# A mixture of experts whose first product keeps the weights in the array and streams the tokens

## The chip, the cores and the metric

The kernel runs on one NeuronCore of a Trainium2 chip. The metric is the device time of one execution in microseconds (us), as the median of several runs. A profile, taken from one further execution, gives the start and duration of every instruction on the core's engines: TensorE (PE, with its weight loads listed apart as PEld), VectorE (DVE), ScalarE (ACT), GpSimd (POOL) and the queue of SyncE that issues DMAs (SP).

## The reference: what is computed

The input `x` is 4 x 1024 tokens of 256 float32 values. Four layers follow one another, each added to `x` after a layer norm: a retention layer (16 heads), a mixture of experts, an RWKV layer (a recurrence over 1024 tokens), and the same mixture again, with the same weights. The change is in the mixture:

```python
logits = t @ Wg.T + bg                      # 4096 tokens, 8 experts
probs = softmax(logits); topw, topi = top_k(probs, 2)
topw = topw / sum(topw)
for e in range(8):
    h = t @ w1[e].T                         # 256 -> 512
    gate, up = split(h, 2)                  # 256 each
    a = silu(gate) * up
    o = a @ w2[e].T                         # 256 -> 256
    out += combine[:, e] * o                # 0 for tokens that did not choose e
```

All of it is float32.

## The kernel before, in words

**Pages.** The kernel computes the mixture only for the experts that a token chose. Each of the 2 x 4096 (token, expert) pairs gets a slot in a table in DRAM (`xg_all`), sorted by expert, in pages of 128 slots; a page belongs to one expert. There are `NSL = 71` pages per mixture: 64 full ones and 7 more, since each expert's last page may be partly empty. `Piece.route` computes the slots on DVE in several steps. `Piece.send` (line 792) normalizes 128 tokens on ACT and writes each of them to its two slots by two indirect DMAs that POOL issues. A mixture is routed in pieces of the batch, and its first `FULL = 25` pages can be worked off before the later pieces have been sent; page 25 and those behind it need every send.

**One page** `j` goes through these steps in class `Moe`:

- `get` (827): SP loads up to four pages of slots into `m_xg`.
- `fetch` (838): PE transposes the page's 128 x 256 tokens in two blocks into `m_xtp` (PSUM), and ACT copies them to `m_xt`, so that channels lie on partitions.
- `expert` (906): PE loads the number of the page's expert from `m_ofi` into a register. In the profile this is TENSOR_LOAD, FUSED_REGOPS and SEQ_ASSERT on PE's queue.
- `up` (848): the first product. The tokens (`m_xt`, two blocks of 128 channels) are the stationary operand, loaded into the array, and the expert's weights, 512 columns of `w1a` that the register points to, are the moving one. `m_hp` has tokens on partitions and the 512 hidden units along the row. ACT takes silu of the first half (`m_sg`), DVE multiplies it by the second half into `m_a`. For the first page of each group of four, DVE also computes from the tags of the slots their shares (`m_share`) and the rows that they go to (`m_to`), in seven small operations.
- `turn` (878): PE transposes `m_a` in two blocks into `m_atp`, and DVE copies it to `m_aT`, so that hidden units lie on partitions.
- `down` (885): the second product, with `m_aT` stationary and 256 columns of `w2a` moving, into `m_op`, which has one PSUM buffer that it shares with another tile (tag `yp`). ACT scales it by the share into `m_y`.
- `scatter` (896): POOL issues an indirect DMA that writes the page's 128 rows to `y_all` in DRAM.

**Order.** `tiles` (909) writes out by hand the order on PE, ACT, DVE and POOL: in iteration `j` it fetches page `j + 2`, does `up(j)`, loads the expert of `j + 1`, turns `j - 2` and does `down(j - 4)`. SP's order is left to a scheduler. `extra[j]` holds work of the neighbouring layers that is put behind iteration `j`: the ends of retention, routing and sends of the later pieces, the inputs of RWKV (from `FULL + 24` on), and, once the pages that hold a block of tokens have been scattered, `ask` (938) and `take` (950): SP loads the two rows of each token from `y_all` into `m_back`, and DVE adds them to `x` (line 954). The functions `back_to` and `add` set their iterations. Scatters are held back in the list `late`: POOL has a budget of seven DMA issues for three iterations, sends go first, and at most `LAG = 8` pages wait (lines 927 to 935). `m_y` has `LAG + 4` buffers.

**Numbers of instructions.** Each float32 matmul of the program stands in the profile as two MATMUL and two LDWEIGHTS; a transpose stands as one of each. So `m_hp` has 142 pages x 2 blocks x 2 = 568, `m_op` 568, `m_atp` and `m_xtp` 284 each.

Of the kernel before, what the change touches and what calls it, by code (L numbers as in the profile page):

```python
# [62 lines left out]
HB = NBLK // 2  # L63
HT = HB * NT
FULL = 2 * HT - E + 1
LAG = 8

W = C + 4
N_OUT = 2 * TT * P
# [40 lines left out]
def hybrid_kernel(  # L110
# [693 lines left out]
    class Moe:  # L804


        def __init__(self, layer, pieces):
            self.layer = layer
            self.xg, self.to, self.ev, self.xt, self.act, self.aT = {}, {}, {}, {}, {}, {}
            self.rows, self.share, self.ofi, self.ofs = {}, {}, {}, []  # L810
            self.y, self.late = {}, []
            self.slots = tc.dram_tile([NSL * P, W], F32, name=f"xg_all{layer}")
            *self.sends, self.early = dram_disjoint_views(self.slots, 2 * TT + 1)
            self.results = tc.dram_tile([N_OUT + NSL * P, C], F32, name=f"y_all{layer}")
            *self.scatters, self.back = dram_disjoint_views(self.results, NSL + 1)
            self.pieces, n = [], 0
            for k in pieces:
                self.pieces.append(Piece(self, n, k, self.pieces[-1] if n else None))
                n += k

            self.groups = [(0, 1)] + [
                (lo, min(GRP, end - lo)) for start, end in ((1, FULL), (FULL, NSL))
                for lo in range(start, end, GRP)]
            self.group = {lo + i: (g, i) for g, (lo, n) in enumerate(self.groups) for i in range(n)}
# [21 lines left out]
            nc.scalar.copy(self.xt[j], tp)  # L846

        def up(self, j):
            hp = psum([P, DFF], "m_hp")
            for c in range(KC):  # L850
                mm(hp, lhsT=self.xt[j][:, c, :],  # L851
                   rhs=w1a[:, bass.ds(self.ev[j], 1), c, :].rearrange("p o n -> p (o n)"),
                   start=(c == 0), stop=(c == KC - 1))
            sg = px.tile([P, C], F32, name="m_sg", tag="m_sg", bufs=2)
            nc.scalar.activation(sg, hp[:, 0:C], AF.Silu)  # L855
            self.act[j] = px.tile([P, C], F32, name="m_a", tag="m_a", bufs=3)
            nc.vector.tensor_mul(self.act[j], hp[:, C : 2 * C], sg)  # L857
            g, i = self.group[j]
            if i == 0:
                n = self.groups[g][1]  # L860
# [14 lines left out]
                    second, tags[:, :, 0], 0.0, second, ALU.is_gt, ALU.mult)  # L875
                nc.vector.tensor_add(to[:, 0:n], second, void[:, j : j + n])

        def turn(self, j):
            tp = px2.tile([P, KC, P], F32, name="m_atp", tag="m_atp", bufs=2)
            for c in range(KC):  # L880
                nc.tensor.transpose(tp[:, c, :], self.act[j][:, c * P : (c + 1) * P], ident)  # L881
            self.aT[j] = px.tile([P, KC, P], F32, name="m_aT", tag="m_aT", bufs=3)
            nc.vector.tensor_copy(self.aT[j], tp)

        def down(self, j):
            op = psum([P, C], "m_op", "yp")
            for c in range(KC):
                mm(op, lhsT=self.aT[j][:, c, :],  # L888
                   rhs=w2a[:, bass.ds(self.ev[j], 1), c, :].rearrange("p o n -> p (o n)"),
                   start=(c == 0), stop=(c == KC - 1))  # L890
            g, i = self.group[j]
            y = self.y[j] = px.tile([P, C], F32, name="m_y", tag="m_y", bufs=LAG + 4)
            nc.scalar.activation(y, op, AF.Copy, scale=self.share[g][:, i : i + 1])  # L893
            self.late.append(j)
# [11 lines left out]
        def expert(self, j):  # L906
            self.ev[j] = nc.tensor.value_load(self.ofi[j], min_val=0, max_val=E - 1)

        def tiles(self, extra):


            spent = 0
            self.fetch(0)
            self.fetch(1)
            self.expert(0)
            for j in range(NSL + 4):
                if j + 2 < NSL:
                    self.fetch(j + 2)
                if j < NSL:
                    self.up(j)  # L920
                if j + 1 < NSL:
                    self.expert(j + 1)
                if 0 <= j - 2 < NSL:
                    self.turn(j - 2)
                if j > 3:
                    self.down(j - 4)
                spent = max(spent, 7 * j // 3)
                for f, *a in extra.get(j, ()):
                    f(*a)
                    spent += 2 * (f.__name__ == "send")  # L930
                while self.late and (spent < 7 * (j + 1) // 3 or len(self.late) > LAG):
                    self.scatter()
                    spent += 1
            while self.late:
                self.scatter()
# [665 lines left out]
    def back_to(moe, pieces):  # L1601

        for p in pieces:
            lo, hi = p.start * NT, p.start * NT + p.nt
            start = 2 * hi + E - 1 + 4
            for i in range(lo, hi):
                add(start + i - lo, moe.ask, i)
                add(start + 2 + i - lo, moe.take, i)
# [25 lines left out]
    add(FULL + 4, inputs)  # L1634
    back_to(moe, moe.pieces[:1])
    for n in range(-1, 8):
        add(FULL + 25 + 3 * n if n >= 0 else FULL + 24, lambda n: made["rwkv"][0](n), n)
    moe.tiles(extra)
    pi, w = made["pi"], made["w"]
    prepare, wstep, finish = made["rwkv"]  # L1640
# [208 lines left out]
```

## Time and profile before

| | |
|---|---|
| median of 3 runs | 1552.75 us (1551.82 to 1554.12) |
| the profiled execution | 1556.23 us |
| its span, first to last instruction | 1554.3 us |
| mean granted TensorE clock | 0.925 |
| first `m_hp` of the first mixture, last of its `m_hp` pages | 346.4, 630.8 us |
| first `m_hp` of the second mixture, last of its `m_hp` pages | 1265.5, 1528.5 us |
| `m_a` on DVE (line 857) | 142 x 423 ns |
| `m_aT` on DVE (line 883) | 142 x 415 ns |
| `y_all` scatter on POOL (line 900) | 142 x 969 ns |
| `xg_all` send on POOL (line 798) | 128 x 978 ns |

How to read it: a line of the profile names the source line, the engine, the operation, the tiles as out<-in, and the count; behind the bar stand busy us and mean ns, and behind the second bar the idle time of that engine just ahead of these instructions, with what ended it. In a timeline the first two numbers are the start and the duration in us, both from the start of the span; what stands in brackets is the idle time ahead and its releaser. A timeline line with x4 covers four instructions, from the start of the first to the end of the last. A stage's line begins with its window and length, has the busy us of PE, PEld, DVE, ACT and POOL with their instructions, and ends with the granted clock, the DMA share and GB/s.

### The profile page before, as it was taken

To read this page: it belongs to the slowest core of one execution; us is meant where nothing else is said; L and a number is where in the kernel's file an instruction comes from. 1 tells how busy PE (TensorE), PEld (TensorE's weight loads), DVE (VectorE), ACT (ScalarE), POOL (GpSimd) and SP (SyncE) were. 2 spreads that over 40 slices of the span, in tenths; PEclk is the share of its full clock that TensorE was granted. 3 is DMA by queue.
4 is the path that set the end of the run, shared out by engine and by line. 5 is a ranking of instruction groups with operands and counts; after the bars stand their busy time and mean duration, and the time that the engine had idled before them with its cause. 6 is when DMAs were issued, how large, how long until landed. Compare 5 with 4: busy or idle time off the path is not lost.

```text
span 1554.3 us, 20957 instructions
## 1 busy us (share of the span) xinstructions
PE 1313.1 (84%) x6704; PEld 675.9 (43%) x6704; DVE 1004.7 (65%) x1963; ACT 648.7 (42%) x1649; POOL 891.2 (57%) x854
## 2 busy tenths in 40 slices
PE   5999998877879999997878888888787567979995
PEld 3666665544445655422222323233222124546663
DVE  6667567426533344399978797989998956433454
ACT  2343434433533334445445454545445234523332
POOL 4232322742564335399998888887799923553332
PEclk9999999878989999999989898999898779989998
DMA  8992111231432341267655453534554831333564
GB/s 296 329 330 74 56 55 42 81 115 53 132 115 87 114 139 62 72 149 195 164 135 149 122 145 99 145 99 122 136 162 136 248 107 48 104 105 99 159 207 159
DMA packets 117546, 207.71 MB, mean 134 GB/s; under 512 B 12192, under 2 KB 80000, under 8 KB 117440
## 3 DMA queue, kind: packets, MB, share of 16 engines
q1 hardware_dynamic: 95904, 160.22, 36.1%
q0 software_dynamic: 17184, 39.86, 8.2%
q10 hardware_dynamic: 4352, 6.29, 1.3%
q8 instruction: 57, 0.93, 0.3%
q14 instruction: 49, 0.40, 0.1%
HBM read 139.19 MB, written 67.14 MB: 133 GB/s over the span
## 4 chain that ended last, share of the span: by engine, by line
PE 57%; DVE 14%; POOL 11%; ACT 8%; issue 5%; DMA 2%; another core or an unknown queue 2%; POOLq 0%; SPq 0%; DVEq 0%; ACTq 0%
PE m_hp L851 15%; PE m_op L888 7%; PE w_pp L1108 5%; POOL w_s L1204 5%; DVE w_s L1196 4%; PE a_qkp L315 3%; PE a_yp L374 2%; DVE w_vb L1194 2%; PE m_xtp L844 2%; PE w_dp L1056 2%; PE a_op L249 2%; PE a_sp L354 2%; PE a_gp L297 2%; PE m_atp L881 2%; POOL w_xf L1074 2%
## 5 line engine op out<-in xcount | busy, mean ns | idle before, releaser
L1204 POOL TENSOR_TENSOR w_s<-w_s,w_rT 128x1024 f32<-128x1024 f32 x128 | 303.9, 2411 | 38.9 <-DVE w_s L1196 27.8
L851 PE MATMUL m_hp<-w1a,m_xt 128*128 x568 | 283.2, 623 | 3.8 <-DVE m_a L857 3.8
L900 POOL DMA_INDIRECT y_all<-m_y,m_to x142 | 137.5, 969 | 211.8 <-ACT m_xt L846 145.4
L857 DVE TENSOR_TENSOR m_a<-m_hp,m_sg 128x256 f32<-128x256 f32 x142 | 60.1, 423 | 266.2 <-ACT m_sg L855 239.5
L798 POOL DMA_INDIRECT xg_all<-m_row,m_at x128 | 125.2, 978 | 100.0 <-ACT m_row L796 42.9
L1196 DVE TENSOR_TENSOR_SCAN w_s<-w_wk,w_carry,w_vb 128x512 f32<-128x512 f32 x128 | 161.0, 1276 | 17.3 <-PE w_yp L1227 5.1
L888 PE MATMUL m_op<-w2a,m_aT 128*128 x568 | 150.8, 389 | 19.5 <-ACT m_y L893 13.7
L1194 DVE TENSOR_TENSOR w_vb<-w_vb,w_wk 128x1024 f32<-128x1024 f32 x128 | 153.3, 1198 | 18.8 <-ACT w_wk L1137 17.6
L1196 DVE TENSOR_TENSOR_SCAN w_s<-w_wk,w_vb 128x512 f32<-128x512 f32 x128 | 152.9, 1216 | 13.2 <-POOL w_sx L1027 3.0
L851 PEld LDWEIGHTS m_hp<-w1a,m_xt 128*128 128x128 f32 x568 | 102.4, 200 | 79.0 <-issue 74.2
L1227 PE MATMUL w_yp<-w_s,core_c 128*32 128x512 f32 x512 | 92.3, 645 | 47.7 <-POOL w_s L1204 38.0
L855 ACT ACTIVATE m_sg<-m_hp 128x256 f32<-128x256 f32 x142 | 54.5, 384 | 169.4 <-PE m_hp L851 119.3
L888 PEld LDWEIGHTS m_op<-w2a,m_aT 128*128 128x128 f32 x568 | 98.7, 194 | 31.5 <-ACT m_y L893 17.2
L893 ACT ACTIVATE m_y<-m_op,m_share 128x256 f32<-128x256 f32 x142 | 67.2, 473 | 107.3 <-PE m_op L888 84.4
L327 POOL TENSOR_TENSOR a_t<-a_t,a_t 128x512 f32<-128x512 f32 x32 | 41.0, 1281 | 118.3 <-DVE a_t L326 95.9
L1074 POOL TENSOR_TENSOR w_xf<-w_xf,w_sx 128x512 f32<-128x512 f32 x60 | 77.8, 1297 | 40.5 <-ACT w_xf L1073 39.5
L357 DVE TENSOR_TENSOR a_pt<-a_sp,ret_c 128x2048 f32<-128x2048 f32 x32 | 73.2, 2286 | 16.9 <-PE a_sp L354 16.9
L881 PEld LDWEIGHTS m_atp<-cst,m_a 128*128 128x128 f32 x284 | 40.6, 144 | 79.6 <-issue 67.8
L1077 POOL TENSOR_TENSOR w_xf<-w_xf,w_xT 128x512 f32<-128x512 f32 x64 | 69.7, 1090 | 5.4 <-DVE w_xf L1071 0.7
L844 PE MATMUL m_xtp<-cst,m_xg 128*128 128x128 f32 x284 | 58.3, 289 | 13.5 <-DMA m_xg<-xg_all 13.3
L846 ACT COPY m_xt<-m_xtp 128x256 f32<-128x256 f32 x142 | 51.9, 366 | 37.8 <-PE m_xtp L844 22.4
L1227 PEld LDWEIGHTS w_yp<-w_s,core_c 128*32 128x32 f32 x512 | 14.2, 113 | 112.4 <-POOL w_s L1204 59.4
(312 smaller groups left out, 2496.7 us busy)
## 6 DMA issues: line engine op xcount, KB each, us to landing
w_vb<-v_all SPq DMA_DIRECT2D x125, 512.0 KB
xg_all<-zero SPq DMA_DIRECT2D x34, 520.0 KB
m_xg<-xg_all SPq DMA_DIRECT2D x34, 520.0 KB
tab<-in_rope SPq DMA_DIRECT2D x32, 512.0 KB
m_back<-y_all SPq DMA_DIRECT2D x48, 256.0 KB
v_all<-w_vT SPq DMA_DIRECT2D x64, 128.0 KB
res<-in_x SPq DMA_DIRECT2D x8, 512.0 KB
w1a<-in_w SPq DMA_DIRECT2D x8, 512.0 KB
```

What stands on the lines that cost most here:

```text
L357: nc.vector.tensor_mul(pts[i].rearrange("p j n t -> p (j n) t"), sp.rearrange("p j n t -> p (j n) t"), causal.unsqueeze(1).to_broadcast([P ...
L798: nc.gpsimd.indirect_dma_start(out=self.moe.sends[2 * (self.start * NT + i) + n][:, :], out_offset=bass.IndirectOffsetOnAxis(ap=self.at[n] ...
L844: nc.tensor.transpose(tp[:, c, :], self.xg[g][:, i, c * P : (c + 1) * P], ident)
L851: mm(hp, lhsT=self.xt[j][:, c, :], rhs=w1a[:, bass.ds(self.ev[j], 1), c, :].rearrange("p o n -> p (o n)"), start=(c == 0), stop=(c == KC - 1))
L888: mm(op, lhsT=self.aT[j][:, c, :], rhs=w2a[:, bass.ds(self.ev[j], 1), c, :].rearrange("p o n -> p (o n)"), start=(c == 0), stop=(c == KC - 1))
L900: nc.gpsimd.indirect_dma_start(out=self.scatters[j][:, :], out_offset=bass.IndirectOffsetOnAxis(ap=self.to[g][:, i : i + 1], axis=0), in_= ...
L1074: nc.gpsimd.tensor_mul(xf, xf, sx)
L1108: mm(pp, lhsT=w[n][:, c, m * P : (m + 1) * P], rhs=d["xf", f][:, c, :], start=(c == 0), stop=(c == KC - 1))
L1194: nc.vector.tensor_mul(vb, vb, wk[:, 1:2, :].to_broadcast([P, 2, BLK]))
L1196: nc.vector.tensor_tensor_scan(s[:, q, 1 : BLK + 1], wk[:, 0, :], vb[:, q, :], 0.0 if j % NB == 0 else st[j - 1]["carry"][:, n, 2 * h + q ...
L1204: nc.gpsimd.tensor_mul(s[:, :, 0:BLK], s[:, :, 0:BLK], d["r"][:, g, :].unsqueeze(1).to_broadcast([P, 2, BLK]),)
L1227: mm(d["yp", g][32 * q : 32 * q + 32, :], lhsT=w["sel"][:, i, :], rhs=d["s", n, q // 2][:, q % 2, 0:BLK], start=False, stop=(i == 3), skip ...
```

## The change

The expert's 256 x 512 weights become the stationary operand of the first product, in eight blocks of 128 x 128, and the page's tokens are streamed. The output `m_hp` then has hidden units on partitions (4 blocks of 128 units x 128 tokens), and `m_a` can go into the second product as it is: `turn`, `m_atp` and `m_aT` are gone. The stationary blocks are read from a copy of the expert's weights at a fixed address: for each page the new `first` loads the expert's number into a register of DVE, and DVE copies that expert's weights, 128 x 1024 float32, from `w1a` into `m_w1` (three buffers). `tiles` calls it for page `j + 2` in iteration `j`, ahead of `up(j)`, and for pages 0 and 1 ahead of the loop. `down` comes two iterations after `up`, not four, and `m_op` gets two PSUM buffers of its own, where `m_atp` had them. `LAG` is 6, so `m_y` has 10 buffers, and the iterations of `ask`, `take` and of RWKV's preparation move two earlier.

```diff
-LAG = 8
+LAG = 6
...
         def up(self, j):
-            hp = psum([P, DFF], "m_hp")
-            for c in range(KC):
-                mm(hp, lhsT=self.xt[j][:, c, :],
-                   rhs=w1a[:, bass.ds(self.ev[j], 1), c, :].rearrange("p o n -> p (o n)"),
-                   start=(c == 0), stop=(c == KC - 1))
-            sg = px.tile([P, C], F32, name="m_sg", tag="m_sg", bufs=2)
-            nc.scalar.activation(sg, hp[:, 0:C], AF.Silu)
-            self.act[j] = px.tile([P, C], F32, name="m_a", tag="m_a", bufs=3)
-            nc.vector.tensor_mul(self.act[j], hp[:, C : 2 * C], sg)
+
+            hp = psum([P, DFF // P, P], "m_hp")
+            for m in range(DFF // P):
+                for c in range(KC):
+                    mm(hp[:, m, :],
+                       lhsT=self.w1[j][:, c, m * P : (m + 1) * P],
+                       rhs=self.xt[j][:, c, :], start=(c == 0), stop=(c == KC - 1))
+            sg = px.tile([P, KC, P], F32, name="m_sg", tag="m_sg", bufs=2)
+            nc.scalar.activation(sg, hp[:, 0:KC, :], AF.Silu)
+            self.act[j] = px.tile([P, KC, P], F32, name="m_a", tag="m_a", bufs=3)
+            nc.vector.tensor_mul(self.act[j], hp[:, KC : 2 * KC, :], sg)
...
-        def turn(self, j):
-            tp = px2.tile([P, KC, P], F32, name="m_atp", tag="m_atp", bufs=2)
+        def down(self, j):
+            op = px2.tile([P, 512], F32, name="m_op", tag="m_op", bufs=2)[:, 0:C]
             for c in range(KC):
-                nc.tensor.transpose(tp[:, c, :], self.act[j][:, c * P : (c + 1) * P], ident)
-            self.aT[j] = px.tile([P, KC, P], F32, name="m_aT", tag="m_aT", bufs=3)
-            nc.vector.tensor_copy(self.aT[j], tp)
-
-        def down(self, j):
-            op = psum([P, C], "m_op", "yp")
-            for c in range(KC):
-                mm(op, lhsT=self.aT[j][:, c, :],
+                mm(op, lhsT=self.act[j][:, c, :],
                    rhs=w2a[:, bass.ds(self.ev[j], 1), c, :].rearrange("p o n -> p (o n)"),
                    start=(c == 0), stop=(c == KC - 1))
...
+        def first(self, j):
+
+            e = nc.vector.value_load(self.ofi[j], min_val=0, max_val=E - 1)
+            self.w1[j] = px.tile([P, KC, DFF], F32, name="m_w1", tag="m_w1", bufs=3)
+            nc.vector.tensor_copy(
+                self.w1[j], w1a[:, bass.ds(e, 1), :, :].rearrange("p o c n -> p (o c) n"))
+
         def tiles(self, extra):
...
             self.expert(0)
-            for j in range(NSL + 4):
+            self.first(0)
+            self.first(1)
+            for j in range(NSL + 2):
                 if j + 2 < NSL:
                     self.fetch(j + 2)
+                if j + 2 < NSL:
+                    self.first(j + 2)
                 if j < NSL:
                     self.up(j)
                 if j + 1 < NSL:
                     self.expert(j + 1)
-                if 0 <= j - 2 < NSL:
-                    self.turn(j - 2)
-                if j > 3:
-                    self.down(j - 4)
+                if j > 1:
+                    self.down(j - 2)
...
-            start = 2 * hi + E - 1 + 4
+            start = 2 * hi + E - 1 + 2
...
-        add(FULL + 25 + 3 * n if n >= 0 else FULL + 24, lambda n: made["rwkv"][0](n), n)
+        add(FULL + 23 + 3 * n if n >= 0 else FULL + 22, lambda n: made["rwkv"][0](n), n)
```

More of the change, by code (lines that the diff above doesn't have):

```diff
@@ L808, in __init__ @@
             self.layer = layer
-            self.xg, self.to, self.ev, self.xt, self.act, self.aT = {}, {}, {}, {}, {}, {}
+            self.xg, self.to, self.ev, self.xt, self.act = {}, {}, {}, {}, {}
             self.rows, self.share, self.ofi, self.ofs = {}, {}, {}, []
-            self.y, self.late = {}, []
+            self.y, self.w1, self.late = {}, {}, []
             self.slots = tc.dram_tile([NSL * P, W], F32, name=f"xg_all{layer}")
```

## The prediction

> **What bounds the kernel now.** I read the page's table of engines first, then its groups, then busy time by stage, then the timeline of one page of the mixture.
>
> ```profile
> PE 1313.1 (84%) x6704; PEld 675.9 (43%) x6704; DVE 1004.7 (65%) x1963; ACT 648.7 (42%) x1649; POOL 891.2 (57%) x854
> ...
> L851 PE MATMUL m_hp<-w1a,m_xt 128*128 x568 | 283.2, 623 | 3.8 <-DVE m_a L857 3.8
> ```
>
> TensorE (PE) is busiest and the edited product, m_hp, is its largest group. The share of the whole span says little, because the middle of the span (RWKV) is not touched. The two mixtures run at 342 to 640 us and 1262 to 1540 us. Their quiet halves are these two windows (after the time, busy us of PE, PEld, DVE, ACT, POOL):
>
> ```profile
> 474.00:640.00 166.00, 163.15 (x607) 94.41 (x608) 69.46 (x236) 63.26 (x159) 70.27 (x81) 0.99 0.31 98
> 1388.00:1540.00 152.00, 148.00 (x587) 91.31 (x585) 71.22 (x240) 55.65 (x148) 49.31 (x52) 1.00 0.48 152
> ```
>
> PE never rests there, at full granted clock (1.00, 0.99), while VectorE (DVE) is under half busy. By the starts of m_hp the windows hold 45 and 47 of the 142 pages. One page on PE's timeline:
>
> ```profile
> 521.16 0.38 PE L881 MATMUL m_atp<-cst,m_a 128*128 128x128 f32 x2
> 521.38 1.03 PE L888 MATMUL m_op<-w2a,m_aT 128*128 x4
> 522.24 0.38 PE L844 MATMUL m_xtp<-cst,m_xg 128*128 128x128 f32 x2
> ```
>
> The difference of starts is the cost, not the printed duration, since matmuls overlap. m_hp runs from 519.44 to 521.16: 1.72 us for 4 instructions, 0.43 each (512 columns). m_atp takes 0.22, m_op 0.86 (0.215 each, 256 columns), m_xtp 0.22 (0.11 each, 128 columns). Sum 3.02, the period of most pages. In the first halves of the mixtures PE waits in places: on route chains through DVE, and on GpSimd (POOL), which issues a send or a scatter every 1.265 us without rest (427 to 470, 1339 to 1385).
>
> **Part by part.**
>
> **Removed: turn.** Two transposes per page, 0.22 us of PE, and DVE's copy m_aT (0.415).
>
> **Changed: the first product.** The same columns stream in 16 instructions of 128 in place of 4 of 512, and each needs a weight load of its own. What one load and matmul cost, back to back, decides. Rows near it:
>
> ```profile
> 253.81 0.97 PEld L385 LDWEIGHTS a_kv<-a_vz,a_t 128*128 128x128 f32 x8 [0.45 <-DVE a_t L326]
> ```
>
> Eight plain 128x128 loads, held up by nothing but each other (their matmuls have 64 columns): (0.97 - 0.19)/7 = 0.111 us per load. The stream of 128 columns takes 0.11 (m_xtp). So a pair costs 0.109 to 0.112 if load and stream run side by side; m_op shows that they do, with its load hidden behind 0.215. I take 0.111: 16 x 0.111 = 1.78 in place of 1.72. The new page is 0.22 + 1.78 + 0.86 = 2.86, that is 0.16 less. It breaks even at (1.72 + 0.22)/16 = 0.121 per pair, a narrow margin. The upper bound is the only chain in which a full plain load meets 128 columns (at full clock):
>
> ```profile
> 254.75 0.66 PE L657 MATMUL m_rank<-m_both,cst 128*128 128x128 f32 x2
> 255.23 0.65 PE L658 MATMUL m_rank<-m_both,cst 128*128 128x128 f32 x2
> ```
>
> 0.24 per pair. I don't take it: m_rank's moving operand is read with a stride (line 652 swaps its axes), and with 32 columns the same code runs a pair in (1299.25 - 1299.04)/2 = 0.105, so the stride makes the time, not the load. The new moving operand, m_xt, is contiguous. 92 quiet pages x 0.164 = **-15.1 us**.
>
> [...]
>
> Issue does not bind: loads and matmuls per page rise from 24 to 44, 15 per us, and the stretch from 100 to 200 us holds 20 per us (1000 matmuls, 999 loads).
>
> **Added on DVE: first.** Per page a register load, and a copy of 128x1024 (the weights of one expert). PE's own register load shows TENSOR_LOAD 0.30, FUSED_REGOPS 0.15, SEQ_ASSERT 0.02 and 0.05 for the address: 0.52. The copy is not in this trace. Copies of 128x8 and 128x320 in SBUF take 0.16 and 0.32, a slope that gives 0.68; a multiply of 128x1024 (L1194) takes 1.20, the upper bound; 0.32 is the lower. I take 0.68. DVE's load at its worst is 24.47 us in 1480 to 1520, 13.2 pages, 1.85 per page; it becomes 1.85 - 0.415 + 0.68 + 0.52 = 2.64 of 2.86. It is hidden: page j+2's copy is issued ahead of page j's multiply and needed two pages on. Behind it on DVE wait that multiply, the route steps and the takes; its own wait, for page j-1 to release the buffer, is over by then since DVE has just multiplied page j-1. In the first halves, where PE waits for route steps on DVE, the cover is thin: up to 1.2 - 0.415 = 0.8 us per step.
>
> **Moved: down, two pages earlier; m_op has two PSUM buffers.** In the drain after the last page, PE waits for m_y to free the one buffer: 0.13 (from the starts) + 0.35 + 0.56 + 0.56 = 1.6 us at 633 to 640, and 0.34 + 0.35 + 0.56 + 0.56 = 1.8 at 1532 to 1538. With two buffers and only two drained pages these go: **-3.4**. The last scatter starts at 1541.14, 2.4 us after its m_y (1538.30 + 0.47), because seven scatters queue on POOL behind the takes' loads (POOL idles 5.89 until 1533.55). The order of scatters and loads against each other is the same after, but more of those pages still come 2.86 apart, so POOL catches up at 1.265: **-2.4**. What is late next is the landing of that scatter and the loads behind it, unchanged.
>
> **First halves: 50 pages.** Best, every page gains 0.16: -8. Worst, nothing is gained where POOL is saturated, and DVE's route steps come later. LAG 6 and down's earlier place put two more scatters between the last sends (2 x 1.265 = 2.5 us later), against PE's gain before them. m_y has 10 buffers for 12, but scatters are forced two earlier, so its margin stays. I take **+3** in all.
>
> Sum: -15.1 - 3.4 - 2.4 + 3 = **-18**. The profiled execution took 1556.23 (span 1554.3), 3.5 above the median of 1552.75; -18 gives 1538 for it and **1535** for the median.
>
> **Rivals.**
>
> **Pair rate.** Load and stream don't overlap for 128 columns, and a pair costs 0.22 to 0.24. The first product then takes 3.5 to 3.8 and a page 4.6 to 4.9: 92 pages x 1.6 = +147 at least, all 142 x 1.9 = +270 at most: **1700 to 1820**. It decides from 0.121. For: the rank rows. Against: m_op, and 32 columns at 0.105. Chance 10%.
>
> **DVE becomes the bound.** If the copy takes 1.20 and the register load 0.7, a page with takes costs DVE 1.85 - 0.415 + 1.9 = 3.34. Some 26 pages (from 1460 on) then run at 3.34 instead of 2.86, +12, and the route steps add some 3 to 8: **1545 to 1558**. Against: the slope of the copies. Chance 16%.
>
> **Copies hold POOL.** [...] The 58 issues of the saturated runs (10, 16, 7, 11, 6, 8) would each wait up to 0.68: +39 at most; one copy per 2.86 us meets an issue with (0.68 + 0.96)/2.86 = 57% and costs half on average, 58 x 0.57 x 0.34 = +11: **1546 to 1574**. For: DVE's tensor_scalar L282 takes 0.40 alone and 1.36 beside POOL's L327. Against, the one issue that meets such a copy:
>
> ```profile
> 490.81 0.98 POOL L900 DMA_INDIRECT y_all<-m_y,m_to  x1 [0.16 <-issue]
> ```
>
> The copy of 128x320 and two tensor_scalars run at 491.12 to 492.04, and the issue takes 0.98 in place of 0.96. Chance 12%. [...]
>
> That the change doesn't do what it says is out: in the built order each page has eight products of 128x128 and no turn.
>
> **How the numbers follow.** Forecast 62%, own range 1520 to 1549; pair rate 10%, DVE 16%, POOL 12%. A measurement of this kernel can tell about 0.2% (3 us) from no change. Faster: 0.61 + 0.08 + 0.04 = 0.73. Same: 0.01 + 0.05 + 0.02 = 0.08. Slower: 0.10 + 0.03 + 0.06 = 0.19. The low end: a pair at 0.109 (-3) and 50 early pages that gain 0.16 instead of +3 (-11) make 1521; another -3 for ends that free more, 1518. The high end, 1562, takes in DVE's case and most of POOL's; the pair rate stays out.
>
> **What would show it.** m_hp's 16 starts 0.11 apart and quiet pages 2.86 apart (a pair at 0.12 or more: step wrong). No wait of PE for m_w1. The copy near 0.68, POOL's issues still 0.96. POOL's last scatter within 0.5 us of its m_y. If the quiet pages are right and the total is not, it went in the first halves.

## The result, and the profile after

The changed kernel takes **1543.52 us** in the median of five runs (1537.25 to 1547.68), the kernel before on the same chip 1552.99 (1551.82 to 1554.12): a ratio of 0.9927, with a 95% interval of 0.9911 to 0.9943. It is 9.5 us faster, where 18 were forecast. Its runs spread over 10 us, those of the kernel before over 2.3. The profiled execution took 1547.68 us with a span of 1545.6, so it stands 8.5 below that of the kernel before (1556.23, span 1554.3); all that follows compares these two.

The first product at the new rate is read from PE's timeline of one quiet page:

```profile
521.07 0.38 PE L844 MATMUL m_xtp<-cst,m_xg 128*128 128x128 f32 x2
521.28 1.95 PE L853 MATMUL m_hp<-m_xt,m_w 128*128 128x128 f32 x16
523.07 1.03 PE L883 MATMUL m_op<-w2a,m_a 128*128 x4
523.94 0.38 PE L844 MATMUL m_xtp<-cst,m_xg 128*128 128x128 f32 x2
```

From 521.28 to 523.07 there are 1.79 us for 16 pairs, 0.112 each, and from one m_xtp to the next 2.87 us. Every plain page of the quiet halves has this period, where it was 3.02. The page of the profile, its table of engines and four groups (behind the first bar busy us and mean ns of one):

```profile
PE 1298.3 (84%) x8124; PEld 810.6 (52%) x8124; DVE 1054.1 (68%) x1963; ACT 646.9 (42%) x1649; POOL 916.1 (59%) x854
...
L853 PE MATMUL m_hp<-m_xt,m_w 128*128 128x128 f32 x2272 | 296.3, 286 | 16.1 <-issue 7.8
...
L895 POOL DMA_INDIRECT y_all<-m_y,m_to x142 | 153.6, 1081 | 208.0 <-ACT m_xt L846 125.3
L798 POOL DMA_INDIRECT xg_all<-m_row,m_at x128 | 130.7, 1021 | 74.0 <-issue 28.8
...
L908 DVE COPY m_w<-w1a 128x1024 f32 x142 | 100.9, 711 | 65.7 <-issue 59.4
```

Loads and matmuls rose from 6704 to 8124 each. The copy takes 0.71 us in the mean, 0.694 in the median. POOL's scatter takes 1.081 where it took 0.969, its send 1.021 where it took 0.978. And m_hp, which had waited for DVE alone, now idles 7.8 us for "issue", that is, for nothing that the profile shows.

Where the 8.7 us of the span come from is seen when both executions are cut at the first m_hp of certain pages:

| from the first m_hp of | before, us | after, us | difference |
|---|---|---|---|
| the span's start to page 0 of mixture 1 | 346.4 | 345.8 | -0.6 |
| page 0 to 24 (first half; sends and routes) | 120.5 | 129.6 | **+9.1** |
| page 24 to 70 (quiet half) | 163.9 | 156.2 | -7.7 |
| page 70 to page 0 of mixture 2 (drain, RWKV) | 634.7 | 628.2 | -6.5 |
| page 0 to 24 (first half) | 124.5 | 132.3 | **+7.8** |
| page 24 to 70 (quiet half) | 138.6 | 131.6 | -6.9 |
| page 70 to the end (drain, last rows) | 25.8 | 21.9 | -3.8 |

The quiet halves and the drains did what was forecast. The first halves lost 17 us: 3.4 of it are only moved, since two products of `down` (0.86 each) now lie ahead of page 24 in each mixture instead of in its drain; the rest is real. In the second mixture it has one place, 1360 to 1381. PE's timeline there:

```profile
1361.18 0.69 PE L853 MATMUL m_hp<-m_xt,m_w 128*128 128x128 f32 x4 [0.46 <-issue]
1362.60 1.08 PE L853 MATMUL m_hp<-m_xt,m_w 128*128 128x128 f32 x3 [0.73 <-issue]
1364.04 0.56 PE L853 MATMUL m_hp<-m_xt,m_w 128*128 128x128 f32 x1 [0.36 <-issue]
1366.14 0.37 PE L853 MATMUL m_hp<-m_xt,m_w 128*128 128x128 f32 x1 [1.54 <-issue]
1367.55 0.37 PE L853 MATMUL m_hp<-m_xt,m_w 128*128 128x128 f32 x1 [1.04 <-issue]
...
1371.74 0.58 PE L883 MATMUL m_op<-w2a,m_a 128*128 x1 [1.72 <-issue]
1374.53 1.50 PE L883 MATMUL m_op<-w2a,m_a 128*128 x2 [2.21 <-issue]
```

Inside one accumulation, where no semaphore stands between two matmuls, PE starts one instruction, at times a few, each 0.70 us or a multiple of it (1361.18, 1362.60, 1366.14, 1367.55; the loads stand between). I call this **the drip**. Two pages take 26.4 us in place of 5.7, the second of them at a granted clock of 0.50 (1365 to 1386). In this half the kernel before had two waits of PE that are gone:

```profile
1367.15 2.07 PE L888 MATMUL m_op<-w2a,m_aT 128*128 x4 [3.93 <-ACT m_y L893]
1383.50 2.08 PE L888 MATMUL m_op<-w2a,m_aT 128*128 x4 [4.14 <-issue]
```

The profile names no releaser for the second, but ACT's `m_y` had ended just ahead of it, at 1383.44. The first mixture has another loss, a wait for rows ahead of page 23, on PE's timeline:

```profile
456.23 1.03 PE L883 MATMUL m_op<-w2a,m_a 128*128 x4
469.73 0.66 PE L844 MATMUL m_xtp<-cst,m_xg 128*128 128x128 f32 x2 [12.47 <-DMA m_xg<-xg_all]
```

Page 25's tokens, fetched two pages ahead, need every send. The same wait was 6.82 us before, and the last send (POOL) started earlier:

```profile
462.21 0.66 PE L844 MATMUL m_xtp<-cst,m_xg 128*128 128x128 f32 x2 [6.82 <-DMA m_xg<-xg_all]
455.75 0.96 POOL L798 DMA_INDIRECT xg_all<-m_row,m_at  x1 [0.30 <-issue]
```

POOL's timeline after shows why:

```profile
457.51 0.96 POOL L798 DMA_INDIRECT xg_all<-m_row,m_at  x1 [0.30 <-issue]
458.78 1.37 POOL L798 DMA_INDIRECT xg_all<-m_row,m_at  x1 [0.31 <-issue]
460.45 0.96 POOL L895 DMA_INDIRECT y_all<-m_y,m_to  x1 [0.30 <-issue]
461.72 0.96 POOL L798 DMA_INDIRECT xg_all<-m_row,m_at  x1 [0.30 <-DMA xg_all<-m_row,m_at]
462.99 0.96 POOL L798 DMA_INDIRECT xg_all<-m_row,m_at  x1 [0.30 <-issue]
464.25 0.96 POOL L895 DMA_INDIRECT y_all<-m_y,m_to  x1 [0.30 <-issue]
```

The last send starts at 462.99, 7.2 us later than before. Thirteen scatters are issued ahead of it, where nine were (in the second mixture ten, where six were); four more at 1.27 us each are 5.1 of the 7.2. An issue beside a copy of DVE takes longer in the mean: of the 206 issues between 340 and 660 and from 1260 on, the 91 that overlap a copy take 1.19 us, the other 115 0.97 (the one at 458.78 takes 1.37, beside a copy that starts at 458.62).

### The profile page after: what moved, and what is told of

It reads as the page before. It is cut to its first block, busy times and chain, and to the rows that moved or that the text cites. A ratio compares the mean times of both kernels' runs of the same rounds, so it can differ in the third digit from the quotient of the medians.

```text
span 1545.6 us, 24180 instructions
## 1 busy us (share of the span) xinstructions
PE 1298.3 (84%) x8124; PEld 810.6 (52%) x8124; DVE 1054.1 (68%) x1963; ACT 646.9 (42%) x1649; POOL 916.1 (59%) x854
## 4 chain that ended last, share of the span: by engine, by line
PE 51%; DVE 17%; POOL 15%; ACT 7%; issue 7%; DMA 3%; DVEq 0%; another core or an unknown queue 0%; POOLq 0%; SPq 0%; ACTq 0%
PE m_hp L853 14%; POOL w_s L1208 6%; PE m_op L883 6%; DVE w_s L1200 5%; PE w_pp L1112 4%; PE a_qkp L315 3%; DVE w_vb L1198 2%; PE a_yp L374 2%; PE m_xtp L844 2%; POOL w_xf L1078 2%; PE a_sp L354 2%; POOL w_xf L1081 2%; PE a_gp L297 2%; PE a_op L249 2%; PE w_dp L1060 2%
## 5 line engine op out<-in xcount | busy, mean ns | idle before, releaser
L853 PE MATMUL m_hp<-m_xt,m_w 128*128 128x128 f32 x2272 | 296.3, 286 | 16.1 <-issue 7.8
L853 PEld LDWEIGHTS m_hp<-m_xt,m_w 128*128 128x128 f32 x2272 | 281.8, 201 | 20.4 <-issue 10.0
L895 POOL DMA_INDIRECT y_all<-m_y,m_to x142 | 153.6, 1081 | 208.0 <-ACT m_xt L846 125.3
L798 POOL DMA_INDIRECT xg_all<-m_row,m_at x128 | 130.7, 1021 | 74.0 <-issue 28.8
L883 PE MATMUL m_op<-w2a,m_a 128*128 x568 | 152.4, 392 | 5.6 <-issue 5.2
L908 DVE COPY m_w<-w1a 128x1024 f32 x142 | 100.9, 711 | 65.7 <-issue 59.4
L883 PEld LDWEIGHTS m_op<-w2a,m_a 128*128 128x128 f32 x568 | 101.3, 199 | 14.6 <-issue 6.0
```

Of the source, the lines that this page charges most:

```text
L798: nc.gpsimd.indirect_dma_start(out=self.moe.sends[2 * (self.start * NT + i) + n][:, :], out_offset=bass.IndirectOffsetOnAxis(ap=self.at[n] ...
L853: mm(hp[:, m, :], lhsT=self.w1[j][:, c, m * P : (m + 1) * P], rhs=self.xt[j][:, c, :], start=(c == 0), stop=(c == KC - 1))
L883: mm(op, lhsT=self.act[j][:, c, :], rhs=w2a[:, bass.ds(self.ev[j], 1), c, :].rearrange("p o n -> p (o n)"), start=(c == 0), stop=(c == KC ...
L895: nc.gpsimd.indirect_dma_start(out=self.scatters[j][:, :], out_offset=bass.IndirectOffsetOnAxis(ap=self.to[g][:, i : i + 1], axis=0), in_= ...
L908: nc.vector.tensor_copy(self.w1[j], w1a[:, bass.ds(e, 1), :, :].rearrange("p o c n -> p (o c) n"))
```

## The experiments

Two theories of the missing half went in. **Sends late**: LAG 6 and the earlier `down` push scatters between the last sends. **Drip**: PE loses 20 us in one place, by chance or by the program. The rivals named ahead (the copy's price on DVE, the copy's price on POOL) were tried beside them.

**e1: the changed kernel once more.**

> The changed kernel once more, nothing edited. Its profiled execution took 1547.68 us, the other four 1537.25 to 1544.78, and its trace has 22 us (1359.0 to 1380.9) in which PE starts a matmul only every 0.7 us with nothing on record that holds it. Theory chance: that stretch belongs to single executions and not to the program; then another profile shows it elsewhere, shorter or not at all, and that execution lies near 1537 to 1543. Theory program: the stretch comes from the order of the instructions (POOL has 18 scatters and 14 sends in that window without rest); then it comes again between 1355 and 1385 and the time is 1543 to 1548. Median expected 1543, ratio to the kernel before 0.993, either way; the 12.5 us gap of PE ahead of page 25 (457 to 470) comes again by both.

It took 1544.43 us (1541.36 to 1551.01), ratio 0.9921 (0.9900 to 0.9942). The drip came again, from 1362.7 to 1383, with more than 20 steps of 0.70 or 1.40 us, and a short one at 457 to 460. So it is the program's. The wait ahead of page 25's rows was 9.4 us; the last send was no earlier (465.88), but the short drip had already made PE late.

**e2: LAG 8 with 10 m_y buffers.**

```diff
-LAG = 6
+LAG = 8
-            y = self.y[j] = px.tile([P, C], F32, name="m_y", tag="m_y", bufs=LAG + 4)
+            y = self.y[j] = px.tile([P, C], F32, name="m_y", tag="m_y", bufs=10)
```

> LAG back to 8 with the 10 m_y buffers kept. Theory sends late: LAG 6 and the earlier down push scatters in among the last sends, so the first page of the second half (FULL) gets its rows 5.6 us later than before; with LAG 8 two scatters (2 x 1.265 us) move behind the last send of each mixture, the gap of PE ahead of page 25 shrinks from 12.5 to some 10 us, and the whole is 1538 to 1541 against 1543.5. Rival buffers: with 10 m_y for up to 8 late pages ACT waits for a scatter to release m_y, and PE for m_op, as in the kernel before (2 to 4 us at each of three places): the gaps move and the time stays, 1542 to 1548. Rival nothing: the last sends wait for the takes of x and not for scatters, gap still 12 to 13 us, time 1543.

It took 1542.89 us, ratio 0.9927 (0.9904 to 0.9951): no difference from the changed kernel can be told. The wait did shrink to 9.79 us, as the theory of late sends has it (11 scatters ahead of the last send, not 13). Page 0 to 24 of the second mixture took 119.9 us in place of 132.3, but page 24 to 70 took 138.1 in place of 131.6, since part of the drip now falls into page 24, which took 8.6 us:

```profile
1382.05 0.27 PE L853 MATMUL m_hp<-m_xt,m_w 128*128 128x128 f32 x1 [1.61 <-issue]
1382.76 0.37 PE L853 MATMUL m_hp<-m_xt,m_w 128*128 128x128 f32 x1 [0.44 <-issue]
```

The profiled execution gained 6 us by it, the median nothing that can be told. The late sends are real and worth little by themselves.

**e3: the copy on ACT.**

```diff
-            e = nc.vector.value_load(self.ofi[j], min_val=0, max_val=E - 1)
+            e = nc.scalar.value_load(self.ofi[j], min_val=0, max_val=E - 1)
-            nc.vector.tensor_copy(
+            nc.scalar.copy(
```

> The copy of an expert's first weights and its register load run on ScalarE (ACT) in place of DVE. Theory port: POOL's issues, 1.08 us mean for scatters and 1.02 for sends in the changed kernel (0.97 and 0.98 before), go back to 0.97, the saturated stretches run at 1.265 us per issue again, and the sends before page 25 land 1 to 3 us sooner: 1538 to 1542. Theory DVE: the route steps wait for copies on DVE (gaps of 2.14 us at 432 and 2.6 more than before at 1328), these go, and another 2 to 4 us with them. Against both: a copy of 128x1024 on ACT will take about 1 us (ACT's 128x256 copies take 0.34 to 0.37, against DVE's 0.42), and ACT writes m_sg and m_y, on which PE waits; ACT has 55 of 152 us busy in the last quiet half, so 1.6 us more per page leave it under 2.7 of 2.87, and where takes and row norms fall it is late: 1545 to 1560.

It took 1545.69 us, ratio 0.9938 (0.9908 to 0.9968), three runs near 1540 and three near 1550. Its page, of one near 1540:

```profile
L895 POOL DMA_INDIRECT y_all<-m_y,m_to x142 | 138.1, 973 | 222.6 <-ACT m_xt L846 98.9
...
L798 POOL DMA_INDIRECT xg_all<-m_row,m_at x128 | 125.7, 982 | 79.8 <-issue 27.2
...
L908 ACT COPY m_w<-w1a 128x1024 f32 x142 | 149.1, 1051 | 19.7 <-issue 9.6
```

POOL's issues are back at 0.973 and 0.982 us. So the copies on DVE are what lengthened them, 142 x 0.108 + 128 x 0.039 = 20 us of POOL in all, and taking these away gained nothing that the total shows (ACT's longer copy may have taken a little back). The drip is there without any copy on DVE (from 1349.7 and again from 1369.9), and so is the wait for rows (9.27 us). By these totals neither price of the copy is where the missing time went, as far as runs that lie 10 us apart can tell.

**e4: the copy twice.** The same copy is made two times over.

> Each page's copy is made twice on DVE (0.69 us more per page, output unchanged). Theory hidden: in pages without takes DVE has room (busy 57 us of 152 in the last quiet half is not true of DVE, which has 87, that is 1.63 of 2.87 per page, plus 0.6 of register load), so the quiet pages stay at 2.87 and only the stretch with takes (some 26 pages) goes to about 3.2, +8 us, and POOL's issues grow by another 0.1 us mean; with the first halves +5 to +10: 1556 to 1562. Theory bound: the copy is already on the path in the first halves (50 pages) and costs there its whole 0.69: +35 us, 1575 to 1580.

It took 1564.09 us, ratio 1.0052 (1.0034 to 1.0071): 20 us more than the changed kernel, between the two theories and close to the first, for 103 us of DVE (204.0 of copies in place of 100.9). The quiet pages of the second mixture keep 2.87 up to 1480; from there, where DVE adds rows (`take`), each fourth page takes 4.0. In the first mixture, page 0 to 24 took 136.8 us in place of 129.6, and pages 49 to 53 took 6 more. The single copy is mostly hidden, with little to spare.

**e5: the old product in 16 instructions.**

```diff
-            for c in range(KC):
-                mm(hp, lhsT=self.xt[j][:, c, :],
-                   rhs=w1a[:, bass.ds(self.ev[j], 1), c, :].rearrange("p o n -> p (o n)"),
-                   start=(c == 0), stop=(c == KC - 1))
+            for m in range(DFF // P):
+                for c in range(KC):
+                    mm(hp[:, m * P : (m + 1) * P], lhsT=self.xt[j][:, c, :],
+                       rhs=w1a[:, bass.ds(self.ev[j], 1), c, m * P : (m + 1) * P].rearrange("p o n -> p (o n)"),
+                       start=(c == 0), stop=(c == KC - 1))
```

> The kernel before with its first product cut into 16 instructions of 128 columns (4 column blocks, same stationary page, same moving weights from the register address); no copies, turn and LAG 8 as before. PE issues as many loads and matmuls as in the changed kernel, plus turn. The quiet page should be 3.02 - 1.72 + 1.78 = 3.08 us (a pair at 0.111), +5 to +6 us over some 90 pages. Theory instruction rate: the drip seen in four traces of the changed product (PE starting one instruction each 0.70 us while POOL issues sends and scatters without rest) comes from PE's many short instructions beside POOL's saturated issue; then it appears here too, between 430 and 470 or 1340 and 1390, and costs 5 to 20 us: 1565 to 1580 in all. Theory order: it comes from LAG 6 and the earlier down (or from the copies); then no 0.70 us spacing here, 1558 to 1563.

It took 1580.13 us (1570.94 to 1589.01) against 1555.97, ratio 1.0155 (1.0102 to 1.0208). Its quiet pages take 3.09, 0.06 to 0.07 more than before, as the pair rate says. That is 142 x 0.065 = 9 us; the kernel lost 24. PE's timeline in its second mixture:

```profile
1380.81 0.27 PE L852 MATMUL m_hp<-w1a,m_xt 128*128 x1 [0.45 <-issue]
1381.54 0.36 PE L852 MATMUL m_hp<-w1a,m_xt 128*128 x1 [0.46 <-issue]
1382.24 0.27 PE L852 MATMUL m_hp<-w1a,m_xt 128*128 x1 [0.34 <-issue]
1382.96 1.08 PE L852 MATMUL m_hp<-w1a,m_xt 128*128 x3 [0.45 <-issue]
1385.09 0.37 PE L852 MATMUL m_hp<-w1a,m_xt 128*128 x1 [1.05 <-issue]
```

The drip is here too. The page takes 19.5 us, but 8.5 of them are a wait for `m_y` behind the drip, of the kind that the kernel before has:

```profile
1396.17 2.07 PE L889 MATMUL m_op<-w2a,m_aT 128*128 x4 [8.51 <-ACT m_y L894]
```

Nothing but the number and size of PE's instructions differs from the kernel before: no copy, no LAG 6, no earlier `down`. The runs spread over 18 us, as the changed kernel's do over 10. This carries the theory: **here the drip comes with the short instructions**.

**e6: LAG 10, two m_w1 buffers.** Beside `LAG = 10` and `bufs=2` for m_w1, `first(j + 2)` moves behind `up(j)`, and the takes come two pages later (`+ 4` in `back_to`).

> The changed kernel with LAG 10 and 14 m_y buffers, paid for by two m_w1 buffers in place of three (the copy for page j+2 is issued behind page j's product), takes two pages later. Theory sends late: four scatters fewer (5 us of POOL) stand ahead of the last send of each mixture than in the changed kernel, two fewer than with LAG 8; the gap ahead of page 25 falls from 12.5 (LAG 6) and 9.8 (LAG 8) to 7 or 8 us, the first half of the second mixture gets 3 to 6 us shorter, and the drip, if it needs POOL without rest, shrinks: 1533 to 1539. Rival: the two m_w1 buffers make PE wait for copies (each copy starts 0.4 to 1 us later in the page), some 0.1 us per page and more where DVE takes: 1545 to 1555.

It took 1563.11 us, ratio 1.0039 (1.0026 to 1.0052), and the rival was right. PE's waits by releaser (us in total, times, longest), first of this kernel, then of the changed one:

```profile
PE m_hp L853 <- DVE m_w L908: 17.7, 12, 5.5
```

```profile
PE m_hp L853 <- DVE m_w L908: 2.1, 1, 2.1
```

The third buffer, and the copy's place ahead of the page's multiply, keep the copy hidden. LAG 10 could not be judged beside that.

**e7: the product alone.** As e6, but LAG 8 with 12 m_y buffers, and `down` four pages behind as before (five m_a buffers, RWKV's steps back in their old places).

> The product alone is changed: w1 stationary from the copy, but down stays four pages behind, LAG 8, 12 m_y buffers, takes and RWKV steps where the kernel before has them; two m_w1 buffers, five m_a. m_op keeps its two PSUM buffers. Theory product: quiet pages 2.87 us as in the changed kernel, -13.5 for 90; the drain at each end is two pages of m_op longer (2 x 2 x 0.86 = 3.4) but the first halves have no scatters moved ahead of sends, gap ahead of page 25 7 to 8 us (6.8 before): 1537 to 1543, as good as the changed kernel or better, so the earlier down gained nothing net. Theory drip by instructions: the 0.70 us spacing is still there in the first half of the second mixture, 5 to 18 us; then 1543 to 1548. Theory drip by order: it is gone, 1533 to 1538.

It took 1563.00 us, ratio 1.0045 (1.0029 to 1.0062); 16.1 us of waits for m_w, as in e6, spoil its total. Two things are still read from it. Nine scatters stand ahead of the last send again, as before, so it is LAG 6 and the earlier `down` that put four more there. The wait ahead of page 25's rows is 7.21 us, near the 6.82 of before, but that does not show what made it 12.5: the last send starts at 462.58, hardly earlier than in the changed kernel, and PE comes to it later, after its waits for m_w1. And the drip (6 steps from 1387.8) is there without LAG 6 and the earlier `down`.

**m1: PE beside POOL, with nothing else.** The stages are made of these two loops, POOL's and PE's, here in short, behind a barrier of all engines.

```python
for k in range(32):
    nc.gpsimd.indirect_dma_start(out=views[k][:, :],
        out_offset=bass.IndirectOffsetOnAxis(ap=at[:, k : k + 1], axis=0), in_=res[1][:, k % 8, :], in_offset=None)
for j in range(14):
    for m in range(4):
        for c in range(2):
            mm(hp[:, m, :], lhsT=wc[:, c, m * P : (m + 1) * P], rhs=xt[:, c, 0:P], start=(c == 0), stop=(c == 1))
    for c in range(2):
        mm(op, lhsT=xt[:, 2 + c, 0:P], rhs=w1a[:, j % E, c, 0:C], start=(c == 0), stop=(c == 1))
```

> Not the reference's computation: x is copied to the output, and eight stages of 14 mixture pages on PE (16 pairs of 128 columns and 4 instructions of 256) stand one behind the other: pairs alone; beside 32 scatters on POOL; with DVE copies too; with six loads of 512 KB on SP too; with PE's register load too; the same with 4 instructions of 512 columns instead of the pairs; pairs with everything but POOL; pairs with the register load alone. A page is 2.64 us with pairs at 0.111, 2.58 with the wide ones. Theory POOL beside pairs: the 0.70 us spacing shows in one of the stages with pairs and scatters, at the latest in the fifth, and in none without scatters and not with the wide product. Theory elsewhere: no stage shows it, 14 pages in 37 us each, so it needs something else of the mixture's first half (semaphore traffic of routes and sends). Scatter issues: 0.96 us without copies, 1.1 to 1.3 with.

Without scatters, 14 pages take 37.0 us (2.65 each), with copies and loads by SP or without (38.5 in the first stage, whose first instructions are slower). Beside 32 scatters (one each 1.268 us, 40 us in all) they take 67.9, 68.3, 68.0 and 68.7, in the second stage already, where nothing else runs. The wide product is not spared, though I had expected it to be: 60.7 us, where 14 pages at the rates of the kernel before (1.72 + 0.86 us) would be 36. Its stall comes later, 18.0 us after POOL's first issue in place of 10.3 to 13.2.

**m2: what it takes.**

> Not the reference's computation: x is copied to the output, and ten stages stand one behind the other. Stages 0 to 5 have 14 mixture pages on PE (2.65 us each when free, 40 loads and matmuls) beside: 32 scatters on POOL without rest; the same with a POOL multiply of 128x512 after each 5; with one of 128x128 after each 5; 32 plain stores of 128 KB issued by POOL; the same 32 stores issued by SP; 16 POOL multiplies of 128x1024 and no DMA. Stage 6 has 22 wide products (8 loads and matmuls in 1.72 us) beside 32 scatters, stage 7 22 products in 128-column pairs (32 in 1.78 us) beside them, stage 8 400 DVE copies of 128x8 beside them, stage 9 the copies alone. Theory supply: while POOL issues without rest PE gets no new instructions, and lives on those it has, about 200 records; then stage 0 stalls after 12 to 14 us for some 27 us as in the run before, stage 7 after 10 to 12 us, stage 6 late (about 35 us, so hardly), and stages 4 and 5 not at all; pauses of 1 us after each 5 issues (stage 1) let PE run on. Rival traffic: the rows that the scatters write crowd PE out; then stage 4 stalls as well. Rival port: POOL at work crowds PE out, then stage 5 stalls as well. If it is only PE, stage 8 takes as long as stage 9.

The first 37 us of stages 0 to 7, in this order (after the time, busy us of PE, PEld, DVE and POOL with their instructions):

```profile
28.00:65.00 37.00, 20.43 (x100) 17.39 (x100) 0.00 (x0) 27.74 (x29) 0.71 0.28 100
99.70:136.70 37.00, 36.94 (x279) 35.58 (x280) 0.00 (x0) 29.83 (x30) 1.00 0.24 86
149.20:186.20 37.00, 22.49 (x120) 19.37 (x120) 0.00 (x0) 29.27 (x33) 0.73 0.27 96
218.00:255.00 37.00, 36.98 (x280) 35.56 (x280) 0.00 (x0) 17.14 (x32) 1.00 0.33 115
255.50:292.50 37.00, 36.95 (x279) 35.58 (x280) 0.00 (x0) 0.00 (x0) 1.00 0.34 115
293.00:330.00 37.00, 36.92 (x279) 35.56 (x280) 0.00 (x0) 35.74 (x16) 1.00 0.00 1
332.00:369.00 37.00, 29.82 (x64) 12.37 (x64) 0.00 (x0) 27.99 (x29) 0.95 0.28 99
387.30:424.30 37.00, 13.25 (x96) 12.57 (x96) 0.00 (x0) 27.88 (x29) 0.75 0.28 99
```

Read the count behind PE: 280 is a stage that PE finishes, 100 or 120 one in which it starves. Plain stores issued by POOL (row 4), the same bytes issued by SP (row 5) and POOL's own computing (row 6) do nothing; so in these stages it is neither traffic nor POOL at work (the plain stores keep POOL issuing for 18 us only, which is longer than the 12 us after which scatters stop PE). Scatters starve PE, unless POOL does something else for 1.28 us after each five (row 2; 0.47 us, row 3, is too little). In the stages with pairs, 0, 2 and 7, PE runs through exactly **160 loads and matmuls** and then stops, after 13.1, 12.3 and 9.2 us. In m1's stages with pairs it was 200, 200, 200 and 160. With wide products it stops after 112 in both measurements, after 18.2 us in m1 and 23.7 in m2, where I had expected it hardly to stop. So a count fits better than a time, but with pairs it is not one number; and the first stop always stands between two pages, at an instruction that has a semaphore to wait for, while later steps fall inside an accumulation as well. DVE is not exempt: its 400 copies take 105.0 us beside scatters and 82.0 alone, with steps of 1.40 us from the 87th on.

This fits the kernels in the main. In the profile of the kernel before, POOL's runs without a rest in the first halves hold 102 to 117 instructions on PE's queues each, and no drip follows. In the changed kernel the 24 issues from 1346.5 to 1376.8 hold 254, and the steps begin after 206. Over all kernels with a drip they begin after 96 to 223, so it isn't one fixed number there, and the lowest lies among the counts of the kernel before.

**e8, e9, e10: rests for POOL.** In the first half of the second mixture, POOL multiplies 128x192 twice after at least seven issues (e8) or five (e9, and e10 again), by calls of this function behind each send and scatter. `m_y` has 9 buffers in place of 10, in both mixtures.

```diff
+        def rest(self, j, issued):
+            if self.layer == 0 or issued < 5 or not 12 <= j <= FULL:
+                return issued
+            t = px.tile([P, 192], F32, name="m_rest0", tag="m_rest0")
+            for k in range(2):
+                nc.gpsimd.tensor_mul(t, w1a[:, 0, k, 0:192], w1a[:, 1, k, 0:192])
+            return 0
```

> The changed kernel, and in the first half of the second mixture (pages 12 to 25) POOL does two multiplies of 128x192 (about 1.2 us, their result unused) after at least 7 sends and scatters; m_y has 9 buffers for 10. Theory supply: PE has instructions for about 160 loads and matmuls (10.4 us at 15 per us) once POOL issues without rest, and 7 issues take 8.9 us; so the drip of 17 to 22 us at 1360 to 1383 goes or shrinks to a few us, the last sends come 3 to 5 us later, and the whole gains 5 to 10: 1534 to 1539 against 1543.5, runs closer together. If the stock isn't full again after 1.2 us, the drip is only later and shorter: 1539 to 1543. Rival: the rests only delay the last sends (4 us), and PE waits for rows instead: 1544 to 1548.

> As the one before, but after at least 5 sends and scatters, the spacing at which the eight-stage stall vanished in the measurement with 32 scatters. Theory supply: no 0.70 us spacing between 1340 and 1390 at all; the last sends 5 to 7 us later than without rests; 1534 to 1540, and the runs within 1.5 us of each other as in the kernel before, since the drip's length is what varied. Rival: 1545 to 1550, PE waits for rows.

> The kernel with rests after at least 5 issues once more. In the last two runs no 0.70 us step stood anywhere, not even in the first mixture, where POOL issued 29 times without a rest, and the kernel before took 1529 us there against 1553 to 1558 in the earlier runs: the chip they ran on does not starve PE, so they told nothing of the rests. If this run's kernel before takes 1553 to 1558 again: theory supply says no steps of 0.70 us in the second mixture's first half, its length (page 0 to 25) 122 to 126 us against 133.7 in the changed kernel, steps still to be found in the first mixture, and 1536 to 1541, ratio 0.988 to 0.991 against 0.9927 and 0.9921. Rival rests too short or too costly: steps at 1340 to 1390 stay, or PE waits 12 us for rows: ratio 0.993 or more. If the kernel before takes 1529 again: ratio 0.995 as in the last run, and nothing more is learnt.

They took 1520.35, 1521.79 and 1519.54 us, but the kernel before took 1528.9 and 1528.8 beside them, not 1553 to 1558. They ran on two other chips than e1 to e7 and the two measurements. The ratios are 0.9936 (0.9917 to 0.9954), 0.9955 (0.9937 to 0.9974) and 0.9941 (0.9924 to 0.9958). Their profiles have no drip even in the first mixture, which has no rests, and where POOL issues 29 times without a pause beside some 340 loads and matmuls. That mixture takes 122.5 us from page 0 to 24, where the changed kernel took 129.6. So the rests had nothing to cure here, and PE had a wait for rows, as its timeline in e8 shows ahead of page 23 of the second mixture:

```profile
1353.81 0.81 PE L883 MATMUL m_op<-w2a,m_a 128*128 x3
1359.77 0.66 PE L844 MATMUL m_xtp<-cst,m_xg 128*128 128x128 f32 x2 [5.16 <-DMA m_xg<-xg_all]
```

Whether rests would gain where the drip is, stays open. So does the change's own worth where the drip is not: there is no run of the changed kernel without rests there, and no profile of the kernel before. No version was found that clearly beats the changed kernel.

## Why the prediction came out as it did

- **Pair rate, the step that carried the sum: right.** 0.112 us per pair against 0.111, a page of 2.87 against 2.86. The quiet halves gave -14.6 against -15.1. Load and stream do not add here: at 0.112 a full load (0.111, the `a_kv` row) and a full stream (0.11, `m_xtp`) lie side by side, where one behind the other would be 0.22.
- **The copy on DVE: right.** 0.69 to 0.71 us against 0.68, and one wait of PE for m_w1, 2.1 us, where none was expected. Two pages near 557 us also cost some 3.5 us, where PE waits for DVE (0.77 and 1.30 us) and then takes 3.00 us for 16 pairs from 559.62, at a granted clock that is 0.50 from 561.0 to 563.4. e6 and e7 show what PE waits for m_w1 when the cover is thinner: 16 to 18 us.
- **Drains: right in size, wrong in part.** -6.5 and -3.8, less the 3.4 that only moved, are -6.9 against -5.8; the first of the two stretches holds the whole RWKV layer as well, so the match is in part luck. PE's waits are gone: the last m_y starts 5.0 us after the first m_hp of page 70, where it took 9.8. But POOL did not catch up. The last scatter starts at 1532.33, 3.1 us after the end of its m_y, not within 0.5; POOL still issues seven in a row at the end. That term (-2.4) should have been about +0.8 (2.4 us behind its m_y before, 3.1 after).
- **First halves, the step that failed: +3 was forecast and +13.5 came** (+16.9 less 3.4). In the second mixture the drip costs 20.7 us (26.4 less two pages of 2.87), against 8.1 us of waits for m_y (3.93 and 4.14) that the changed kernel does not have; whether the second m_op buffer or the earlier scatters removed them, no run separates. In the first mixture the wait for rows grew by 5.65; three pages (4, 8, 10) took 4.2 more, two of them between 396 and 414, where the granted clock was 0.72 and had been 1.00; three (14 to 16) took 4.3 more, with the wait for m_w1 of 2.1 in them; and a wait for m_y of 4.34 went. The prediction had the late sends in it, as two more scatters ahead of the last send, 2.5 us. There were four more, and the send came 7.2 us later: this term was mis-sized. The prediction named the first halves as the place to look. It had not the drip; "issue does not bind" was argued from 100 to 200 us, where POOL issues no scatters.
- **Copies hold POOL: the effect is there and harmless.** A scatter takes 1.081 us in the mean in place of 0.969, and 0.973 once the copy is on ACT (e3). The one issue that I took as evidence against (0.98) was a poor sample: the 91 beside a copy take 0.96 to 1.57. But POOL's time was not the bound that mattered.
- **DVE the bound: wrong for one copy**, right for two (1564).

What the drip is worth in the comparison of the two kernels is not settled. The old product cut small (e5) loses some 15 us beyond the pair rate, but in its profile only 8.6 us of that lie in the first halves, with other waits among them. Where the drip is missing, the kernel before is 25 us faster as well, and the changed kernel with rests is 7 to 9 us ahead of it, no more than where the drip is. What the kernels lose elsewhere (in the changed kernel, PE was 4 to 7 us later at page 0 already) no run took apart. So the drip is shown as a place where the changed kernel loses time and the forecast did not; that the forecast would have come true without it is not shown.

## What to carry to other kernels

Price a change of tile shape by the starts of back-to-back instructions; that was right to 0.01 us per page. Then count instructions per us in each stretch, and look for what else issues there: cutting one product into four times as many pieces cost 0.07 us a page in the quiet pages, and in the changed kernel 20 us in one place where POOL issued indirect DMAs without a pause. And before moving a step ahead in a hand-written order, list what stands behind it on a saturated queue, since the last item there, here the last send, sets a wait far from the edit.

## What the runs showed of the hardware

- While POOL issues indirect DMAs back to back (one each 1.268 us), PE starts 160 or 200 loads and matmuls (112 with 512 columns; m1 and m2) and stops; then it starts single ones or short bursts 0.70 us or a multiple apart, until 2 to 6 us after the end of POOL's last issue (3.1 in the changed kernel, from 1377.78 to 1380.87). 14 pages take 68 us in place of 37 (m1). DVE shows the same quantum (m2: copies start 0.70 and 1.40 us apart, and 400 take 105.0 us in place of 82.0). What is held back, no run tells. The DMA queue that the page lists as "instruction" moved 67 packets of 16 KB in the changed kernel and 57 before, and 250 instructions start on PE's queues from one to the next in the median (252.5 before). In the changed kernel two of them started at 1349.4 and 1383.2, and the drip lies between them; what the one has to do with the other, no run shows.
- It is not everywhere: in e8 to e10, on two other chips, there was none, not even in the mixture without rests, and the kernel before took 1529 us in place of 1553 to 1558. Whether the chip makes the difference, no run tells.
- In m2, POOL's plain store of 128 KB takes 0.54 us to issue and does not stop PE; the indirect one takes 0.96.
- Copying 128x1024 float32 in SBUF takes 0.69 us on DVE (median, changed kernel) and 1.05 on ACT (mean, e3).
